# Fifth chunk of the keys by block products inside the product with V, in nine more batches

## The chip, the cores and the metric

One core of one Trainium2 chip. The metric is the device time in microseconds of one execution of the whole program on that core. The kernel before took 913.3 us (median of three runs, 913.17 to 913.3). PE is TensorE, DVE VectorE, ACT ScalarE, POOL GpSimd, SP SyncE, whose queue issues most DMAs.

## What is computed

Cross-attention of 16 batches with 100 queries of 640 columns (8 heads of 80), on 718 keys of 384 columns, plus a second attention over 4 extra tokens. Cut to what matters:

```python
query = hidden_states @ Wq
keyt = enc @ Wk                      # 718 keys, 384 -> 640
valt = enc @ Wv
hs = _mha(query, keyt, valt)         # softmax over 718 keys, 8 heads
ca_q1 = einsum('btc,th->bch', ca, Wq_ca)[:, indices, :]
ca_hs1 = _mha(ca_q1, residual, residual)
ca_hs2 = _mha(ca_hs1 @ Wq, ca @ Wk_ca, ca @ Wv_ca)
out = (hs + ca_hs2) @ Wout + b_out + residual
```

All of it is float32.

## The kernel before

One loop runs over the batches b = 0 to 15. The order of the instructions in it is written by hand for every engine; each engine takes its own queue in order and waits by semaphores.

A batch in PE's order: the scores of b in three thirds (`scores`, L784; tile `st[0..2]`, two key blocks of 120 by 800 columns each), the tokens' product z (`softmax2`, L1026), then the keys of batch b + 1 (`Keys`, four of the five chunks of 128 columns) and the values of b (`Values`) by block products that need fewer multiplications (Strassen-like: 15 products in place of 18, on sums of the inputs that POOL makes in `enc_sums` and on sums of the weights). Their results go from the PSUM banks to `kT` and `vs`: the first to reach a place is copied by ACT, the later ones are added by DVE (L421, L423).

The fifth chunk of the keys (columns 512 to 639, `kT[:, 4]`) is made in two ways:

- `last_keys(b + 1)` (L720): nine plain products of 128x128 by 240 columns (3 thirds of the keys, 3 chunks of 128 of the 384), L702, into a two-bank tile, and two ACT copies. This is used in nine batches: 0, 1, 2, 4, 6, 8, 10, 12 and 14.
- `Chunk(b + 1)` (L730): the 15 block products, each only 64 columns wide, in the eight steps of `K4_PLAN` (L117). Two of a step stand in the two halves of the PE array's columns and run side by side; only the product D stands alone, cut into two halves of 120 keys. Bank `one` holds A (upper half) and B (lower half), bank `two` holds C, D and E. A bank's sum is read after a product and the next product is added on top of it, so that each product has to wait for the read of its bank. `move` (L748) reads with an ACT copy when nothing stands at the place yet, else with a DVE addition. This is used in MIXED batches (3, 5, 7, 9, 11, 13), where steps stand between the queries' products and three of them inside the product with V, before (g, n) = (0, 6), (0, 18) and (1, 6).

The product with V (L1698 to L1723) runs in two halves g of four heads; n counts the 24 pairs (head, key block) of a half, with two products each. In half 0 the pairs are sorted by third, so that `st[0]` is used for n = 0 to 7, `st[1]` for 8 to 15 and `st[2]` from 16 on. The bank `a_ps` is then divided by the sum of the exponentials in its last column (`rs`, L1728, L1730) and the tokens' part `hs2` is added (L1737). y_ps (L969), the tokens' product of batch b + 2, follows on PE; DVE copies `g` from it (L983), ACT then `y_sb` (L987). The next batch's scores follow; the middle third takes the banks of `a_ps` and, as its fourth, that of y_ps.

The softmax of the tokens (`softmax1`, L1009) works on `e1` of the next batch in the stages of `Maximum` (L874): transpose, quad, side, mx, spread, over, then the subtraction `less`; `softmax1(n)` does n stages of these. With `scalar` the stage spread is done by ACT (two copies, L917) and mx needs two operations in place of four, with `fine` side and mx are stages of their own. `exponentials1` is ACT's exponential of `e1`.

In batches 3, 6, 8, 11 and 13 (those behind a batch in PAIRS) the output projection of two row blocks is done first, `project_pair` (L1244): nine products in 18 matmuls, DVE reads (`read`, L1272) and three POOL operations (L1280, L1283, L1284), whose results the last two groups of products use. POOL does the tokens' `values2` (L1101, L1108) before them.

Of the kernel before, what the change touches and what calls it, by code (L numbers as in the profile page):

```python
# [8 lines left out]
F32 = mybir.dt.float32  # L9
# [6 lines left out]
NH, D = 8, 80  # L16
# [125 lines left out]
def kernel(  # L142
# [56 lines left out]

    def scores_tile(name):  # L200
        return main.tile([P, 2, ROWS], F32, tag="st", name=name, bufs=NP)

# [115 lines left out]
    )  # L318
    halves = [t[:, u] for t in [scores_tile(f"wq_{i}") for i in range(NP)] for u in range(2)]
    room = halves.pop()  # L320
# [409 lines left out]
    class Chunk:  # L730


        def __init__(self, b, enc):
            self.enc = enc
            one, two = psum1(f"k4_psA_{b}"), psum1(f"k4_psC_{b}")
            half = P // 2
            self.at = {
                "A": [(one, 0, 0, 0, KT)],
                "B": [(one, half, 0, 0, KT)],
                "C": [(two, half, 0, 0, KT)],  # L740
                "D": [(two, i * half, KT, i * KN, KN) for i in range(2)],
                "E": [(two, 0, 0, 0, KT)],
            }
            self.one = one
            self.plan = iter(K4_PLAN)
            self.opened, self.begun = set(), set()
# [37 lines left out]
    def scores(b, g, tiles):  # L784
# [59 lines left out]
        for i, step in enumerate(steps):  # L844
            step(i == 1)
        st = scores_tile(f"st_{b}_{g}")[:n]
        if g == 1:
# [100 lines left out]
    class Second:  # L948
# [173 lines left out]
    class Last:  # L1122
# [121 lines left out]
        def project_pair(self, between):  # L1244
# [29 lines left out]
            product(b1, [(one[:, :2], w(0, 0))], True)  # L1274
            between(1)
            read(b1, 0, 0)
# [181 lines left out]
    for b in range(B):  # L1458
# [44 lines left out]
        st.append(scores(b, 0, tiles))  # L1503
        if b == 0:
            now.exponentials1()
        nc.vector.tensor_tensor(most[:KN], st[0][:, 0], st[0][:, 1], ALU.max)
        st.append(scores(b, 1, tiles))
# [12 lines left out]
        if b == 0:  # L1520
# [22 lines left out]
            less = subtract(2)  # L1543
            exponential(2)
# [5 lines left out]
            second.softmax1(4)  # L1550
        elif b + 1 < B:
# [69 lines left out]
            if not late:  # L1621
                subtract(2)
                exponential(2)
            if not mixed:
                last_keys(b + 1, enc)
            if b + 2 < B:
# [3 lines left out]
            if last.b in PAIRS:  # L1630
                if not mixed:
                    second.softmax1(3)
                last.project_pair(second.softmax1 if mixed else lambda n: None)
                if last.b == max(PAIRS):
# [3 lines left out]
                    )  # L1638
            if not mixed:
                second.softmax1(8)  # L1640
# [50 lines left out]
        held = b in MIXED and not second.less  # L1691
        if 0 < b < B - 1 and not held:
            second.exponentials1()

        mine.hs = hs = hs_sb
        hs2 = now.hs2
        mixed = b in MIXED
        a_pss = [psumk(f"a_ps_{b}_{g}") for g in (1, 0)][::-1] if mixed else None  # L1698
        for g in range(2):
            a_ps = a_pss[g] if mixed else psum1(f"a_ps_{b}_{g}")  # L1700
            a_v = a_ps[:S, : 4 * (D + 1)].rearrange("p (h e) -> p h e", e=D + 1)

# [3 lines left out]
            for n, (h, i) in enumerate(order):  # L1706
                if mixed and (g, n) in ((0, 6), (0, 18), (1, 6)):
# [7 lines left out]
                for lo, hi in QC:  # L1715
# [7 lines left out]
                    )  # L1723
            if b == 0 and g == 1:
                second.softmax1()
                second.exponentials1()
            rs = small.tile([S, 4], F32, tag="rs", name=f"rs_{b}_{g}")
            nc.vector.reciprocal(rs.unsqueeze(2), a_v[:, :, D : D + 1])  # L1728
            cols = slice(4 * g * D, 4 * (g + 1) * D)
            nc.vector.tensor_tensor(  # L1730
                hs[:S, cols].rearrange("p (h d) -> p h d", h=4),
                a_v[:, :, :D],
                rs.unsqueeze(2).to_broadcast([S, 4, D]),
                ALU.mult,
            )
            if b:
                nc.vector.tensor_tensor(hs[:S, cols], hs[:S, cols], hs2[:, cols], ALU.add)  # L1737
        mine.hs2 = hs2
# [65 lines left out]
```

## Time and profile before

| | before |
|---|---|
| median of the runs | 913.3 us (913.17 to 913.3) |
| the profiled execution's own time | 913.33 us |
| its span | 911.6 us |
| granted TensorE clock | 1.0 |
| L702, nine stretches in the loop | 3.65 us each |
| block products L760, six MIXED batches | 192 matmul records |

The profile gives one execution. A float32 product leaves two records on PE. Rows of a view in order of time begin with start and duration in microseconds; rows of groups end with busy time in us, mean ns of one, and idle time before them with what ended it.

### The profile page before, as it was taken

The page shows a single profiled execution, that of the slowest core. Times are in us where ns is not written, and L with a number is a line of the kernel's source. Part 1 is how long each engine was busy: PE and PEld are TensorE (multiplying, and loading weights), DVE is VectorE, ACT ScalarE, POOL GpSimd, SP SyncE. Part 2 cuts the span into 40 slices and gives each one's busy share as a digit, 9 for nine tenths or more (in the row PEclk, how much of TensorE's full clock was granted, in tenths as well). Part 3 has the DMA queues.
Part 4 walks back from the last instruction along what each step waited for, and adds up shares of the span by engine and source line. Part 5 has one row for each costly group of instructions (what it writes and reads, how often), then busy time and mean ns, then how long its engine had stood idle before and what let it go on. Part 6 is the DMA issues. An engine that isn't in the chain of part 4 may idle for free.

```text
span 911.6 us, 28003 instructions
## 1 busy us (share of the span) xinstructions
PE 904.9 (99%) x12046; PEld 755.5 (83%) x12046; DVE 719.5 (79%) x1174; ACT 455.0 (50%) x874; POOL 711.5 (78%) x684
## 2 busy tenths in 40 slices
PE   9999999999999999999999999999999999999998
PEld 6988889797797978888798787988879788797966
DVE  3669795989859898785988869889895898849883
ACT  2244533747437473653737436374743737436441
POOL 8587999787878879696896959958897688977623
PEclk9999999999999999999999999999999999999999
DMA  8822111031301202130121301103230031300110
GB/s 268 283 81 68 48 50 50 30 100 53 111 4 47 84 34 73 55 104 32 48 61 54 104 33 53 55 25 106 53 83 32 24 107 53 97 31 29 56 50 34
DMA packets 50583, 62.96 MB, mean 69 GB/s; under 512 B 13682, under 2 KB 37810, under 8 KB 50460
## 3 DMA queue, kind: packets, MB, share of 16 engines
q1 hardware_dynamic: 48812, 59.18, 21.3%
q8 instruction: 95, 1.56, 0.7%
q10 hardware_dynamic: 1024, 1.15, 0.4%
q0 software_dynamic: 624, 0.85, 0.4%
q14 instruction: 28, 0.23, 0.1%
HBM read 55.59 MB, written 5.57 MB: 67 GB/s over the span
## 4 chain that ended last, share of the span: by engine, by line
PE 96%; DVE 2%; DMA 0%; ACT 0%; issue 0%; ACTq 0%; DVEq 0%
PE a_ps L1716 12%; PE s_ps L799 12%; PE v_psA L450 11%; PE v_psB L450 9%; PE k_psA L481 9%; PE k_psB L481 7%; PE o_ps L1261 5%; PE kT_ps L702 4%; PE v_psC L450 4%; PE k_psC L481 3%; PE q_ps L618 2%; PE q_ps L560 2%; PE v_psD L450 2%; PE v_psE L450 2%; PE k_psA L760 2%; PE v_ps L391 1%
## 5 line engine op out<-in xcount | busy, mean ns | idle before, releaser
L997 POOL TENSOR_TENSOR e<-ca,g 100x800 f32<-100x800 f32 x64 | 99.3, 1563 | 92.5 <-ACT kT L423 53.9
L516 POOL TENSOR_TENSOR enc<-enc 128x240 f32<-128x240 f32 x144 | 113.2, 796 | 11.6 <-DMA enc<-in_enct 4.5
L1480 DVE TENSOR_TENSOR st<-st,over 120x1600 f32<-120x1600 f32 x48 | 119.0, 2482 | 0.0
L1716 PEld LDWEIGHTS a_ps<-vs,st 120*36 120x36 f32 (+3 forms) x3072 | 111.7, 125 | 5.8 <-issue 3.4
L1716 PE MATMUL a_ps<-vs,st 120*36 120x81 f32 (+3 forms) x3072 | 114.7, 233 | 0.0
L450 PE MATMUL v_psA<-wv_sb,enc 128*120 128x320 f32 x352 | 109.3, 433 | 0.0
L1108 POOL TENSOR_TENSOR hs<-hs,hs 100x640 f32<-100x640 f32 x48 | 94.8, 1975 | 3.8
L1101 POOL TENSOR_TENSOR hs<-vb,p 100x640 f32<-100x640 f32 x64 | 90.7, 1428 | 8.7 <-issue 4.7
L481 PE MATMUL k_psA<-enc,wk_sb 128*128 128x240 f32 x384 | 95.2, 370 | 0.1
L1004 POOL TENSOR_TENSOR e<-e,e 100x800 f32<-100x800 f32 x48 | 91.8, 1913 | 3.8
L450 PE MATMUL v_psB<-wv_sb,enc 128*120 128x320 f32 x296 | 91.8, 433 | 0.0
L1488 ACT ACTIVATE st<-st 120x1600 f32<-120x1600 f32 x48 | 73.9, 1539 | 33.9 <-DVE st L1480 33.6
L450 PEld LDWEIGHTS v_psA<-wv_sb,enc 128*120 128x120 f32 x352 | 64.2, 183 | 25.0 <-DVE vs L421 0.5
L481 PEld LDWEIGHTS k_psA<-enc,wk_sb 128*128 128x128 f32 x384 | 71.6, 190 | 16.0 <-DVE wk_sb L546 0.5
L1492 DVE TENSOR_TENSOR most<-most,st 120x800 f32<-120x800 f32 x64 | 67.0, 1047 | 14.9 <-ACT st L849 13.7
L481 PE MATMUL k_psB<-enc,wk_sb 128*128 128x240 f32 x320 | 78.0, 366 | 0.3 <-DVE sm L1083 0.3
L799 PE MATMUL s_ps<-qp,kT 64*64 64x100 f32 (+1 forms) x3072 | 73.1, 248 | 0.0
L450 PEld LDWEIGHTS v_psB<-wv_sb,enc 128*120 128x120 f32 x296 | 54.1, 183 | 21.9 <-DVE vs L421 0.4
L799 PEld LDWEIGHTS s_ps<-qp,kT 64*64 64x64 f32 (+1 forms) x3072 | 66.9, 130 | 5.4 <-issue 4.2
L1176 ACT COPY hsT<-turned_hs 32x160 f32<-32x160 f32 (+7 forms) x244 | 67.7, 278 | 3.0
L481 PEld LDWEIGHTS k_psB<-enc,wk_sb 128*128 128x128 f32 x320 | 60.7, 190 | 8.6 <-issue 0.7
L423 ACT COPY vs<-v_psA 120x640 f32<-120x640 f32 x45 | 31.2, 693 | 65.1 <-PE v_psA L450 64.9
(209 smaller groups left out, 1897.7 us busy)
## 6 DMA issues: line engine op xcount, KB each, us to landing
vb<-va_d SPq DMA_DIRECT2D x62, 250.0 KB
enc<-in_enct SPq DMA_DIRECT2D x30, 240.0 KB
enc<-in_enct SPq DMA_DIRECT2D x15, 360.0 KB
xT<-in_xt SPq DMA_DIRECT2D x8, 500.0 KB
rest<-in_enct SPq DMA_DIRECT2D x31, 120.0 KB
xn<-in_x SPq DMA_DIRECT2D x11, 320.0 KB
out<-xn SPq DMA_DIRECT2D x11, 320.0 KB
ca<-in_cas SPq DMA_DIRECT2D x16, 156.2 KB
```

What stands on the lines that cost most here:

```text
L450: nc.tensor.matmul(at[0][j][:KN, : H // 2], a_form(self.enc, f)[:, j * KN : (j + 1) * KN], wv_there.get(f, wv_sb[:, W_AT[f]]), start=first ...
L481: nc.tensor.matmul(at[:, i * KT : (i + 1) * KT], wk_sb[:, W_AT[f], i], a_form(self.enc, f), start=(first and i == 0), stop=last, skip_grou ...
L516: nc.gpsimd.tensor_tensor(out, left, right, op)
L799: nc.tensor.matmul(s_ps[at][k0:k1, cols], w, rhs, start=not begun & {(at, k) for k in range(k0, k1, 32)}, stop=last, skip_group_check=True,)
L997: first = nc.gpsimd.tensor_tensor(to, self.ca[:, t, :].unsqueeze(1).to_broadcast([S, NH, S]), g[:, :, t].unsqueeze(2).to_broadcast([S, NH, ...
L1004: made = nc.gpsimd.tensor_tensor(e, e, to, ALU.add)
L1101: first = nc.gpsimd.tensor_tensor(to, self.vb[t][:S].rearrange("p (h d) -> p h d", h=NH), p2[:, :, t].unsqueeze(2).to_broadcast([S, NH, D] ...
L1108: nc.gpsimd.tensor_tensor(sums, sums, to, ALU.add)
L1176: nc.scalar.copy(self.hsT(r)[32 * m : 32 * m + 32, :, first - lo : end - lo], turned[32 * i : 32 * i + 32, :, m, first - at : end - at],)
L1480: return nc.vector.tensor_tensor(st[i], st[i], top.over[:KN].unsqueeze(1).to_broadcast([KN, 2, ROWS]), ALU.subtract,)
L1488: nc.scalar.activation(st[i], st[i], AF.Exp, scale=SCALE)
L1716: nc.tensor.matmul(a_v[lo:hi, h % 4], st[i // 2][: KEYS[i], i % 2, h * S + lo : h * S + hi], block(i, h // 4)[: KEYS[i], h % 4], start=(i ...
```

## The change

The fifth chunk is made by `Chunk` in the nine other batches too. PLAIN names six of these, 0, 2, 4, 10, 12 and 14; the rest are 1, 6 and 8. Two steps of the plan stand before the product with V and six in it, at n = 9, 14, 19, 23 of half 0 and n = 3 and 16 of half 1. The first two steps are swapped in these batches, so that D comes first. Around it:

- In PLAIN batches the exponential of `st[2]` stands behind the first two steps, the stages of `softmax1` between the later ones, and the head sums of both halves behind them; the rest of `softmax1` comes after y_ps and `exponentials1` in the next batch, behind its first scores. `softmax1` there has `scalar` and `fine`.
- In batches 6 and 8 (and the MIXED ones behind a pair, as before) `project_pair` calls `softmax1` between its products; the first of the calls is made only in MIXED batches. The later stages follow the projection. In 1, 6 and 8 `exponentials1` stands at the last step.
- In all batches but 15 `a_ps` is in the pool of banks psumk. From batch 1 on, division and addition are one fused operation for each head (100x80), eight of them in place of two multiplications and two additions.
- The three score tiles are fixed tiles; rows 96 to 127 of the first are filled with the lowest number once, so that the maximum runs over 128 rows and ACT's copy of `low` in every batch (L1502) is gone.

```diff
+PLAIN = [b for b in range(B - 1) if b not in (1, *MIXED) and b - 1 not in PAIRS]
...
+    sts = [main.tile([P, 2, ROWS], F32, name=f"st_{i}") for i in range(NP)]
...
-            self.plan = iter(K4_PLAN)
+            swap = b - 1 not in MIXED
+            self.plan = iter(K4_PLAN[1::-1] + K4_PLAN[2:] if swap else K4_PLAN)
...
+                after = self.b - 1
                 self.top = Maximum(
-                    e1, f"1_{self.b}", self.b - 2 in PAIRS, self.b - 1 in MIXED
+                    e1,
+                    f"1_{self.b}",
+                    after - 1 in PAIRS or after in PLAIN,
+                    after in (*MIXED, *PLAIN) or after - 1 in PAIRS,
                 )
...
             product(b1, [(one[:, :2], w(0, 0))], True)
-            between(1)
+            if self.b + 1 in MIXED:
+                between(1)
             read(b1, 0, 0)
...
+        st.append(scores(b, 0, tiles))
+        if b == 0 or b - 1 in PLAIN:
+            now.exponentials1()
         most = wide(f"most_{b}")
-        nc.scalar.copy(most[96:], low[96:].to_broadcast([P - 96, ROWS]))
...
             if not late:
                 subtract(2)
+            if not late and b not in PLAIN:
                 exponential(2)
-            if not mixed:
-                last_keys(b + 1, enc)
...
             if last.b in PAIRS:
-                if not mixed:
-                    second.softmax1(3)
-                last.project_pair(second.softmax1 if mixed else lambda n: None)
+                last.project_pair(second.softmax1)
...
-            if not mixed:
+            if not mixed and b not in PLAIN:
                 second.softmax1(8)
...
+        if b < B - 1 and not b in MIXED:
+            chunk = Chunk(b + 1, enc)
+            chunk.go(2)
+        if b in PLAIN:
+            exponential(2)
...
+        a_pss = [(psumk if b < B - 1 else psum1)(f"a_ps_{b}_{g}") for g in (1, 0)][::-1]
...
+        if b in MIXED:
+            steps = (0, 6), (0, 18), (1, 6)
+        else:
+            steps = (0, 9), (0, 14), (0, 19), (0, 23), (1, 3), (1, 16)
...
+                if b in PLAIN and (g, n) in ((0, 23), (1, 6)):
+                    second.softmax1(1)
+                if b in PLAIN and (g, n) == (1, 16):
+                    second.softmax1(1)
+                if b < B - 1 and (g, n) in steps:
                     chunk.go()
+                    if b not in MIXED and (g, n) == steps[-1]:
+                        if b in PLAIN:
+                            second.softmax1(2)
+                        else:
+                            second.exponentials1()
...
+                for h in range(4):
+                    part = slice((4 * g + h) * D, (4 * g + h + 1) * D)
+                    nc.vector.scalar_tensor_tensor(
+                        hs[:S, part],
+                        a_v[:, h, :D],
+                        rs[:, h : h + 1],
+                        hs2[:, part],
+                        ALU.mult,
+                        ALU.add,
+                    )
...
+        if b in PLAIN:
+            second.softmax1()
```

More of the change, by code (lines that the diff above doesn't have):

```diff
@@ L318 @@
     )
-    halves = [t[:, u] for t in [scores_tile(f"wq_{i}") for i in range(NP)] for u in range(2)]
+    halves = [t[:, u] for t in sts for u in range(2)]
     room = halves.pop()
@@ L845, in scores @@
             step(i == 1)
-        st = scores_tile(f"st_{b}_{g}")[:n]
+        st = sts[g][:n]
         if g == 1:
@@ L1500 @@
             now.softmax1()
-        most = wide(f"most_{b}")
-        nc.scalar.copy(most[96:], low[96:].to_broadcast([P - 96, ROWS]))
[L1503 to L1506, printed above, removed]
+            nc.scalar.copy(
+                sts[0].rearrange("p a r -> p (a r)")[96:],
+                low[96:].to_broadcast([P - 96, 2 * ROWS]),
+            )
+        st.append(scores(b, 0, tiles))
+        if b == 0 or b - 1 in PLAIN:
+            now.exponentials1()
+        most = wide(f"most_{b}")
+        nc.vector.tensor_tensor(most, sts[0][:, 0], sts[0][:, 1], ALU.max)
         st.append(scores(b, 1, tiles))
@@ L1549 @@
             enc_sums(enc_next)
-            second.softmax1(4)
         elif b + 1 < B:
@@ L1691 @@
         held = b in MIXED and not second.less
-        if 0 < b < B - 1 and not held:
+        if b in MIXED and not held:
             second.exponentials1()
+        if b < B - 1 and not b in MIXED:
[3 more added lines that the diff above has]
+            exponential(2)
         mine.hs = hs = hs_sb
         hs2 = now.hs2
-        mixed = b in MIXED
-        a_pss = [psumk(f"a_ps_{b}_{g}") for g in (1, 0)][::-1] if mixed else None
+        a_pss = [(psumk if b < B - 1 else psum1)(f"a_ps_{b}_{g}") for g in (1, 0)][::-1]
+        a_vs = [
+            a_ps[:S, : 4 * (D + 1)].rearrange("p (h e) -> p h e", e=D + 1)
+            for a_ps in a_pss
+        ]
+        if b in MIXED:
+            steps = (0, 6), (0, 18), (1, 6)
+        else:
+            steps = (0, 9), (0, 14), (0, 19), (0, 23), (1, 3), (1, 16)
         for g in range(2):
-            a_ps = a_pss[g] if mixed else psum1(f"a_ps_{b}_{g}")
-            a_v = a_ps[:S, : 4 * (D + 1)].rearrange("p (h e) -> p h e", e=D + 1)
+            a_v = a_vs[g]
             order = [(h, i) for h in range(4 * g, 4 * g + 4) for i in range(len(KC))]
@@ L1723 @@
                     )
[L1724 to L1737, printed above, removed]
+            if b in PLAIN and g == 0:
+                continue
+            for g in range(2) if b in PLAIN else (g,):
+                a_v = a_vs[g]
+                rs = small.tile([S, 4], F32, tag="rs", name=f"rs_{b}_{g}")
+                nc.vector.reciprocal(rs.unsqueeze(2), a_v[:, :, D : D + 1])
+                cols = slice(4 * g * D, 4 * (g + 1) * D)
+                if b == 0:
+                    nc.vector.tensor_tensor(
+                        hs[:S, cols].rearrange("p (h d) -> p h d", h=4),
+                        a_v[:, :, :D],
+                        rs.unsqueeze(2).to_broadcast([S, 4, D]),
+                        ALU.mult,
+                    )
+                    continue
+                for h in range(4):
[5 more added lines that the diff above has]
+                        hs2[:, part],
+                        ALU.mult,
+                        ALU.add,
+                    )
         mine.hs2 = hs2
```

5 lines of the change are left out of this document (removed).

## The prediction

> **What bounds the kernel.** The page first: span, engines, chain of waits.
>
> ```profile
> span 911.6 us, 28003 instructions
> PE 904.9 (99%) x12046; PEld 755.5 (83%) x12046; DVE 719.5 (79%) x1174; ACT 455.0 (50%) x874; POOL 711.5 (78%) x684
> PE 96%; DVE 2%; DMA 0%; ACT 0%; issue 0%; ACTq 0%; DVEq 0%
> ```
>
> TensorE (PE) is busy for 99% of the span and makes 96% of the chain: hardly anything that another engine does shows now. So a product removed is worth its whole time, and every wait that the change puts into PE's queue costs its whole length. Then the chain in order of time, where one of the nine batches (batch 4) has:
>
> ```profile
> 300.98 3.65 PE kT_ps L702 x18
> 304.63 6.91 PE a_ps L1716 x191
> ```
>
> The fifth chunk of the next batch's keys takes 3.65 us, then come the products with V. The instructions of the same batch by engine, in order of time:
>
> ```profile
> 300.82 1.38 PE L702 MATMUL kT_ps<-enc,wk 128*128 128x240 f32 x6
> 304.56 6.98 PE L1716 MATMUL a_ps<-vs,st 120*64 120x81 f32 x192
> 311.36 0.93 PE L969 MATMUL y_ps<-m,xT 128*36 128x72 f32 x20
> 312.21 1.60 PE L799 MATMUL s_ps<-qp,kT 64*64 64x100 f32 x64
> 313.74 1.63 PE L799 MATMUL s_ps<-qz,kT 32*120 32x200 f32 x32
> ...
> 301.02 0.56 ACT L423 COPY kT<-k_psA 128x480 f32<-128x480 f32 x1
> 302.67 1.54 ACT L1488 ACTIVATE st<-st 120x1600 f32<-120x1600 f32 x1 [1.09 <-DVE st L1480]
> 313.44 0.37 ACT L987 COPY y_sb<-y_ps 100x256 f32<-100x256 f32 x1 [2.41 <-DVE g L983]
> ...
> 299.71 2.87 DVE L1480 TENSOR_TENSOR st<-st,over 120x1600 f32<-120x1600 f32 x1
> 302.50 1.00 DVE L890 STREAM_TRANSPOSE turned<-e 128x800 f32<-128x800 f32 x1
> 303.53 0.99 DVE L892 TENSOR_REDUCE quad<-turned 128x25 f32<-128x800 f32 x1
> 304.56 0.71 DVE L895 TENSOR_REDUCE side<-quad 32x25 f32<-32x25 f32 x4
> ```
>
> The 3.65 us of L702 hold nothing that waits, and they cover VectorE's subtraction (to 302.58) and ScalarE's exponential (to 304.21), which the products with st_2 need. That cover goes.
>
> **What the block products cost.** Batch 3 already does its fifth chunk this way:
>
> ```profile
> 246.73 0.38 PE L760 MATMUL k_psC<-enc,w_sums 128*64 128x120 f32 x4
> 246.94 1.86 PE L651 MATMUL q_ps<-xT,wq_sb 128*64 128x200 f32 x20
> 256.87 0.37 PE L760 MATMUL k_psA<-enc,w_sums 128*64 128x240 f32 x1
> 257.28 1.87 PE L1716 MATMUL a_ps<-vs,st 120*64 120x81 f32 x48
> 258.98 0.57 PE L760 MATMUL k_psA<-enc,w_sums 128*64 128x240 f32 x4
> ...
> 246.95 0.72 ACT L752 COPY kT<-k_psA 64x240 f32<-64x240 f32 x2 [2.87 <-PE k_psA L760]
> 247.68 0.52 ACT L752 COPY kT<-k_psC 64x120 f32<-64x120 f32 x2
> 257.49 0.36 ACT L752 COPY kT<-k_psA 128x240 f32<-128x240 f32 x1 [0.84 <-PE k_psA L760]
> ...
> 259.60 0.83 DVE L750 TENSOR_TENSOR kT<-k_psA,kT 64x240 f32<-64x240 f32 x2 [1.31 <-PE k_psA L760]
> ```
>
> A pair takes 256.87 to 257.28, 0.41 us; D takes 0.21. Seven pairs and D: 3.04 (at 0.405, as L702's 3.65 for nine products gives for one) against 3.65: **0.61 less in each of nine batches, -5.5 us**. Between two pairs 48 records take 1.70, so one (h, i) of the products with V (four records) takes 0.142. The Trainium skill ("TensorEngine Tiling (Array Packing)", Key Properties) says that a change of tiling mode drains TensorE; the rows do not show it, since pair and 48 records together keep 2.10 from 256.87 to 258.98, but it is a rival below.
>
> What a read costs a pair behind it, from the same rows: a copy starts 0.62 after its pair's start (256.87 to 257.49) and takes 0.36, an addition starts as late (258.98 to 259.60) and takes 0.42. With some 0.05 to return (an estimate: ScalarE starts that long after a matmul record's end), PE may reuse the bank 1.03 to 1.08 after the pair's start. The L702 way had two copies behind nine products; now there are 14 reads, and each bank is written again after a few (h, i).
>
> **Batch 4 laid out**, T = 300.82. D and the first pair end at T+0.62, nine (h, i) at 1.89. There step (0, 9) writes bank B, which ScalarE must have copied: it is busy with k_psA to T+0.76, then copies D (0.52) and A, B (0.72), to 2.00: PE waits 0.15. (0, 14) comes at 3.16 and finds its addition done; the exponential, now behind the four copies, ends at 3.55, before (h, i) 16 at 3.85; (0, 19) at 4.28 just fits. (0, 23) follows 0.41 and four (h, i) later, 0.97 after (0, 19), but A's addition needs 1.08: wait 0.11. (1, 3) is 0.97 behind (0, 23), whose copy needs 1.03: wait 0.06. (1, 16) is late enough. Products with V end at T+10.2, against 10.54 before (311.36). So **step waits: 0.17 in each of nine batches and about 0.15 more in the six where ScalarE still has work in front (1, 2, 4, 10, 12, 14; batch 0 below): +2.4 us**; bounds 1.2 (half of it) and 3.5.
>
> VectorE now does the tokens' maximum in pieces between the additions: transpose to T+6.4, quad to 8.9, side to 9.6, two additions of the last step to 10.4, two mx to 11.1. Only then come the head sums of both halves, two reciprocals (as short as the first row below, 0.2 each) and eight fused operations of 100x80, which no row shows:
>
> ```profile
> L983 DVE COPY g<-y_ps 100x32 f32<-100x32 f32 x15 | 2.7, 178 | 0.0
> L750 DVE TENSOR_TENSOR kT<-k_psA,kT 64x240 f32<-64x240 f32 x24 | 9.7, 402 | 8.3 <-PE k_psA L760 7.8
> ```
>
> So each costs 0.18 to 0.40; by size nearer the short one, I take 0.22. A price for it is in the Trainium skill ("Vector Engine (DVE) Microarchitecture Reference", 5.2 Measured stream behaviour on trn2): 75 ns and 1.04 ns per column, an estimate of 0.16, by which the next term would be about 0.5. Head sums end at T+13.3, the copy of g and then y_sb (0.37) at 13.85. Scores of batch 5 want y_ps's bank again at its second third's fourth bank: before, at 312.21 + 1.53 + 0.78 + 0.3 = 314.8, 3.4 after the products with V, now T+13.6: wait 0.3 in 2, 4, 10, 12. Batch 14 has no y_ps in between, its head sums are wanted 0.85 earlier: 0.85. **+2.0 us**; bounds 0.5 (at 0.18) and 9 (at 0.40).
>
> **Batches 6 and 8.** Before:
>
> ```profile
> 402.80 1.38 PE L702 MATMUL kT_ps<-enc,wk 128*128 128x240 f32 x6
> 406.44 2.85 PE L1261 MATMUL o_ps<-wout_sb,hsT 128*128 128x320 f32 x10
> 416.23 6.98 PE L1716 MATMUL a_ps<-vs,st 120*64 120x81 f32 x192
> ...
> 406.28 0.65 DVE L904 TENSOR_REDUCE mx<-side 32x25 f32<-32x100 f32 x2
> 416.33 0.89 DVE L1272 TENSOR_TENSOR xn<-o_ps,xn 128x320 f32<-128x320 f32 x2 [0.58 <-PE o_ps L1261]
> ...
> 407.35 1.73 ACT L917 COPY spread<-mx 64x800 f32<-64x800 f32 x2
> ...
> 409.24 0.73 POOL L1280 TENSOR_TENSOR hsT<-hsT,hsT 128x256 f32<-128x256 f32 x1
> 411.20 1.54 POOL L1284 TENSOR_TENSOR wout<-wout,wout_sb 128x640 f32<-128x640 f32 x1
> ```
>
> Two things move. First, between(1) and between(2) now do transpose, quad and side inside the pair projection, but mx and spread come out of softmax1(8) behind it: on VectorE behind the reads of the last o_ps (0.2 + 0.89 after its products), mx 0.65, then the spread on ScalarE 1.73, and only behind that in ScalarE's queue the chunk's copies (0.52 + 0.72). They end 4.8 after the chunk's start; step (0, 9) wants them at 1.9. **Wait 2.9, twice: +5.8 us**, by the order of the queues alone. Second, the projection starts 3.65 earlier, GpSimd does not: L1284 can follow L1280 (409.24) and L1283 at best to 412.2, while the last two products of the projection, 18 of equal length in 9.7, would start at 402.85 + 8.6 = 411.5. **Wait 0.7, twice: +1.4**; bounds 0 and 2.
>
> **Batch 0.**
>
> ```profile
> 85.41 1.38 PE L702 MATMUL kT_ps<-enc,wk 128*128 128x240 f32 x6
> ...
> 86.46 0.64 DVE L421 TENSOR_TENSOR kT<-k_psC,kT 128x480 f32<-128x480 f32 x1
> ...
> 86.07 1.54 ACT L1488 ACTIVATE st<-st 120x1600 f32<-120x1600 f32 x1
> ```
>
> The chunk's first pair takes the bank of k_psC, read until 87.1, and ScalarE is at an exponential until 87.6, then come the copies, 1.24: step (0, 9) at 88.9 instead of 87.4. **+1.5**.
>
> Removed: ScalarE's copy of low and the separate additions of hs, all beside PE: nothing. The rest tile is free earlier, its DMA may land earlier: nothing. Restart of PE behind each of some 35 waits: 0 to 0.14 (no row shows one), I take 0.03: **+1.0**, bounds 0 and 4.9.
>
> **Sum**, against this execution's own time of 913.33 us (span 911.6 and 1.7 around it; the median of the runs is 913.3): -5.5 + 2.4 + 2.0 + 5.8 + 1.4 + 1.5 + 1.0 = +8.6, **922.0 us**.
>
> **Rivals.** (a) Only the queue-order waits remain (6, 8 and 0); the small ones are met, as my 0.05 to 0.15 margins may be too strict: -5.5 + 5.8 + 1.5, 915.1. For it: the 1.08 against 0.97 is a tenth of a us. Against: it recurs in nine batches. (b) Other side: the copies are not late. Place: ScalarE's queue at step (0, 9); from the point where they end within 1.9 of the chunk's start the reads keep pace everywhere and the whole 5.5 stays: 907.8. Against: in 6 and 8 the spread in front ends at 3.6 by measured durations. (c) VectorE's lateness is carried on: behind a plain batch the tokens' second transpose and subtraction, two operations of L890's kind, stand in front of the next batch's maxima, one of them no longer under the products with V, so these come some 1 us later; where additions of the odd batch then hold a bank, six times up to 1.2 us: 929. Against it, in batch 5 VectorE waits for PE and can catch up:
>
> ```profile
> 331.65 0.82 DVE L421 TENSOR_TENSOR vs<-v_psA,vs 120x640 f32<-120x640 f32 x1 [0.58 <-PE v_psA L450]
> ```
>
> (d) The drain by the skill's rule: at 0.16 (a record's 0.37 less half a pair's 0.41) at both sides of six steps in nine batches, +17, 939; the 2.10 above speak against it.
>
> **Chances.** Forecast 0.58, (a) 0.19, (b) 0.06, (c) 0.14, (d) 0.03. The range 914.8 to 928.5 takes in (a) and the lower bounds of the terms, and part of (c). About 0.2% (1.8 us) can be told from no change: faster 0.06 is (b); same 0.07 is the lower part of (a); slower 0.87.
>
> **What would show it.** In batches 6 and 8 PE stands idle for about 3 us before L761's second products, released by ScalarE's copy L753; a stall there missing breaks the forecast. Short waits before L761 at (0, 23) and (1, 3), released by VectorE and ScalarE; a wait of s_ps on y_sb behind 2, 4, 10 and 12; the products L761 themselves 3.04 a batch. PE's share of the span falls below 99%. If it does not, (b) holds.

## Result and profile after

The changed kernel takes 926.79 us (median of four runs, 924.97 to 927.56), the kernel before 913.23 on the same chip: ratio 1.0147, 95% interval 1.0129 to 1.0164. It is slower by 13.6 us; the forecast was 922.0, slower by 8.6, with a range of 914.8 to 928.5.

The page of after, the lines that answer to those shown of before (span, busy time of the engines, chain of waits):

```profile
span 925.8 us, 28438 instructions
PE 911.2 (98%) x12172; PEld 749.1 (81%) x12172; DVE 723.0 (78%) x1288; ACT 462.5 (50%) x907; POOL 703.9 (76%) x684
PE 85%; POOL 7%; DVE 5%; ACT 1%; DMA 1%; issue 1%; ACTq 0%; DVEq 0%; POOLq 0%
```

PE's share of the chain falls from 96% to 85%: other engines now show. PE's busy time even rises, from 904.9 to 911.2, although products were removed. The records did not get longer: the products with V are 3072 records of 233 ns on average before and 234 after, and yet their busy time goes from 114.7 to 126.9. A record starts some 0.035 us behind the last one and runs on for 0.23, so a stretch that is cut into more pieces counts the end of each piece, and a wait shorter than a record counts as busy. Nine batches with six cuts each make 54 more ends of some 0.2 us, 11 of the 12 us. So busy time can't price the change, and places have to be compared. The table does so: time from a batch's first score record to that of the next (for batch 15 to the end of the span), less the same time in the profile of before (the last column is a control, explained with its run below).

| batch | after | 6, 8 as before | subtraction late | x load first | y ahead | steps apart | plain only | all four | before, x load late |
|---|---|---|---|---|---|---|---|---|---|
| 0 | 3.10 | 3.07 | 3.07 | 0.98 | 3.09 | 2.83 | -0.20 | 0.77 | 1.95 |
| 1 | 0.52 | 0.52 | 0.53 | 0.53 | 0.62 | -0.04 | -0.11 | -0.01 | -0.11 |
| 2 | -0.26 | -0.15 | -0.11 | -0.13 | -0.27 | -0.22 | -0.37 | -0.39 | 0.08 |
| 3 | 0.67 | 0.78 | 0.52 | 0.63 | 0.08 | 0.83 | 0.36 | 0.91 | 0.07 |
| 4 | -0.27 | -0.10 | -0.26 | -0.26 | -0.27 | -0.52 | -0.51 | -0.51 | 0.01 |
| 5 | 0.41 | 0.42 | 0.39 | 0.40 | 0.00 | 0.69 | 0.23 | 0.20 | 0.12 |
| 6 | 5.27 | 0.60 | 1.02 | 5.42 | 5.41 | 3.76 | -0.02 | 0.51 | -0.01 |
| 7 | -0.40 | -0.41 | -0.03 | -0.40 | -0.40 | -0.41 | -0.41 | 0.36 | -0.41 |
| 8 | 4.34 | 0.20 | 1.12 | 4.30 | 4.37 | 3.83 | 0.01 | 0.49 | 0.00 |
| 9 | -0.16 | -0.17 | 0.14 | -0.16 | -0.16 | -0.17 | -0.17 | -0.16 | -0.16 |
| 10 | -0.26 | -0.23 | -0.26 | -0.26 | -0.22 | -0.51 | -0.51 | -0.51 | 0.00 |
| 11 | 0.41 | 0.25 | 0.42 | 0.50 | 0.63 | 0.58 | 0.32 | 0.79 | -0.01 |
| 12 | -0.26 | -0.26 | -0.26 | -0.16 | -0.26 | -0.52 | -0.52 | -0.51 | 0.00 |
| 13 | 0.57 | 0.47 | 0.50 | 0.47 | 0.42 | 0.95 | 0.27 | 0.59 | 0.09 |
| 14 | -0.27 | -0.27 | -0.27 | -0.27 | -0.27 | -0.53 | -0.52 | -0.52 | -0.01 |
| 15 | 0.57 | 0.55 | 0.57 | 0.84 | 0.55 | 0.83 | 0.82 | 0.86 | -0.08 |

Four things are to be seen in the column of after: batches 6 and 8 lose 9.6 us of the 14.2 by which the span grew; batch 0 loses 3.1; a plain batch gains 0.26, and the odd batch behind it loses 0.41 to 0.67, more than that.

A plain batch in order of time, batch 4 of after (start, duration; PE, then VectorE, then ScalarE):

```profile
305.10 0.43 PE L761 MATMUL k_psC<-enc,w_sums 128*64 128x120 f32 x4
305.35 0.57 PE L761 MATMUL k_psA<-enc,w_sums 128*64 128x240 f32 x4
305.76 1.43 PE L1739 MATMUL a_ps<-vs,st 120*64 120x81 f32 x36
307.02 0.37 PE L761 MATMUL k_psC<-enc,w_sums 128*64 128x240 f32 x1
...
309.73 0.74 PE L1739 MATMUL a_ps<-vs,st 120*64 120x81 f32 x16
310.38 0.42 PE L761 MATMUL k_psA<-enc,w_sums 128*64 128x240 f32 x1
...
317.66 2.03 PE L800 MATMUL s_ps<-qz,kT 32*120 32x200 f32 x32
...
315.06 0.65 DVE L905 TENSOR_REDUCE mx<-side 32x25 f32<-32x100 f32 x2
...
317.28 0.93 DVE L1764 SCALAR_TENSOR_TENSOR hs_sb<-a_ps,rs,hs 100x80 f32<-100x80 f32 x4
318.12 0.18 DVE L984 COPY g<-y_ps 100x32 f32<-100x32 f32 x1
...
318.33 0.37 ACT L988 COPY y_sb<-y_ps 100x256 f32<-100x256 f32 x1 [0.86 <-DVE g L984]
```

Step (0, 9) at 307.02 waits for nothing: nine (h, i) took 1.26, 0.14 each. At (0, 23) 16 records fill 0.65 instead of 0.57 (four at 0.142): a wait of 0.08, and the pair that had to wait takes 0.46 (310.38 to 310.84, where a pair takes 0.41). At (1, 3) the same shows: 0.06 of waiting and a pair of 0.46. Then the scores: 32 records of `qz` take 2.03 where before they took 1.63. In their stretch y_sb is read until 318.70; that is the 0.40 that batch 5 loses, all of it at this one place. The eight fused operations take 0.93 for four, 0.23 each (0.22 was taken); by the price of the Trainium skill ("Vector Engine (DVE) Microarchitecture Reference", 5.2 Measured stream behaviour on trn2) that the prediction quotes it would be 0.16, so here the measurement decides against it.

Batch 6 of after, same view and columns, with the idle time before a row and what ended it in brackets:

```profile
416.66 1.34 PE L1266 MATMUL o_ps<-wout,hsT 128*128 128x320 f32 x4 [0.42 <-POOL wout L1290]
417.94 0.43 PE L761 MATMUL k_psC<-enc,w_sums 128*64 128x120 f32 x4
...
421.85 0.62 PE L761 MATMUL k_psC<-enc,w_sums 128*64 128x240 f32 x2 [1.82 <-ACT kT L753]
422.60 0.56 PE L761 MATMUL k_psA<-enc,wk 128*64 128x240 f32 x1
...
424.24 0.66 PE L761 MATMUL k_psA<-enc,w_sums 128*64 128x240 f32 x1
...
419.53 1.73 ACT L918 COPY spread<-mx 64x800 f32<-64x800 f32 x2 [10.00 <-DVE mx L905]
421.28 0.52 ACT L753 COPY kT<-k_psC 64x120 f32<-64x120 f32 x2
421.82 0.72 ACT L753 COPY kT<-k_psA 64x240 f32<-64x240 f32 x2
...
418.85 0.65 DVE L905 TENSOR_REDUCE mx<-side 32x25 f32<-32x100 f32 x2
421.29 1.01 DVE L926 STREAM_TRANSPOSE over<-spread 128x800 f32<-128x800 f32 x1 [1.79 <-ACT spread L918]
422.33 1.41 DVE L1024 TENSOR_TENSOR e<-e,over 100x800 f32<-100x800 f32 x1
423.78 0.41 DVE L751 TENSOR_TENSOR kT<-k_psA,kT 64x240 f32<-64x240 f32 x1
```

This is the stall that the prediction named: ScalarE's spread stands in front of the chunk's copies. PE idles 1.82 at step (0, 9), released by L753; the second product of the step needs the second copy, starts at 422.60, and is 2.7 late, where 2.9 was foretold. But the stall does not end there. The addition of the pair's sums starts only at 423.78, behind the tokens' second transpose and subtraction on VectorE, so the next step starts at 424.24, 5.6 us after the start of the products with V (418.60) where it needs 2.4: 3.2 late. In batch 8 it is the same (535.56 to 541.20).

Batch 6 has a second loss that batch 8 lacks. The granted clock drops to half, from 422.73 for 3.41 us, and a record of the block products takes up to 0.66 in place of 0.37. Three microseconds of after, then the same of the run with the steps further apart, below (start:end, length, busy time of PE, PEld, DVE, ACT and POOL, granted clock, DMA):

```profile
423.00:426.00 3.00, 3.00 (x36) 2.62 (x34) 1.81 (x4) 0.00 (x0) 2.84 (x4) 0.50 0.03 8
423.00:426.00 3.00, 2.67 (x53) 2.20 (x52) 1.62 (x5) 0.00 (x0) 2.84 (x5) 1.00 0.03 8
```

From the chunk's start to the last product with V batch 6 takes 14.65 and batch 8, at full clock, 13.71; so some 0.9 to 1.0 of the 5.27 is the clock. The two runs below that also have the drop there (x load first, y ahead) lose 5.4 in batch 6 and 4.3 to 4.4 in batch 8; the run without it (steps apart) loses 3.8 in both. What sets the drop off was not tried; the profile of before has none in the loop.

And batch 0, ahead of the chunk. First before (SyncE's queue, VectorE, GpSimd), then after (the same, and PE):

```profile
39.65 0.52 SPq L218 DMA_DIRECT2D xT<-in_xt  x1
47.18 0.31 SPq L959 DMA_DIRECT2D ca<-in_cas  x1
...
67.34 3.23 DVE L1492 TENSOR_TENSOR most<-most,st 120x800 f32<-120x800 f32 x2
...
67.56 4.41 POOL L997 TENSOR_TENSOR e<-ca,g 100x800 f32<-100x800 f32 x2 [0.56 <-issue]
```

```profile
47.37 0.31 SPq L960 DMA_DIRECT2D ca<-in_cas  x1
47.73 0.38 SPq L218 DMA_DIRECT2D xT<-in_xt  x1
...
67.72 4.98 DVE L1498 TENSOR_TENSOR most<-most,st 120x800 f32<-120x800 f32 x2
...
68.79 3.04 POOL L998 TENSOR_TENSOR e<-ca,g 100x800 f32<-100x800 f32 x2
...
77.02 1.05 PE L481 MATMUL k_psA<-enc,wk_sb 128*128 128x240 f32 x4 [1.64 <-DVE kT L421]
```

The planner that orders the work ahead of the loop put the load of x behind that of `ca`, which waits for GpSimd; the load now comes at 47.73 and not at 39.65. GpSimd's product starts 1.2 us later, VectorE's two maxima take 4.98 in place of 3.23, and PE waits 1.64 at 77.02. Nothing in the diff speaks of this load.

### The profile page after: what moved, and what is told of

The parts are those of the page before. It is cut to its first block, busy times and chain, and to the rows that moved or that the text cites. A ratio compares the mean times of both kernels' runs of the same rounds, so it can differ in the third digit from the quotient of the medians.

```text
span 925.8 us, 28438 instructions
## 1 busy us (share of the span) xinstructions
PE 911.2 (98%) x12172; PEld 749.1 (81%) x12172; DVE 723.0 (78%) x1288; ACT 462.5 (50%) x907; POOL 703.9 (76%) x684
## 4 chain that ended last, share of the span: by engine, by line
PE 85%; POOL 7%; DVE 5%; ACT 1%; DMA 1%; issue 1%; ACTq 0%; DVEq 0%; POOLq 0%
PE s_ps L800 11%; PE a_ps L1739 10%; PE v_psA L450 9%; PE v_psB L450 8%; PE k_psA L481 7%; PE k_psB L481 6%; PE k_psA L761 4%; PE o_ps L1266 3%; PE v_psC L450 3%; PE k_psC L481 2%; PE q_ps L618 2%; PE q_ps L560 2%; PE v_psD L450 2%; PE v_psE L450 2%; PE v_ps L391 1%; PE q_psA L618 1%
## 5 line engine op out<-in xcount | busy, mean ns | idle before, releaser
L1739 PEld LDWEIGHTS a_ps<-vs,st 120*64 120x64 f32 (+3 forms) x3072 | 122.2, 125 | 10.5 <-issue 0.8
L1739 PE MATMUL a_ps<-vs,st 120*64 120x81 f32 (+3 forms) x3072 | 126.9, 234 | 0.0
L516 POOL TENSOR_TENSOR enc<-enc 128x240 f32<-128x240 f32 x144 | 106.8, 752 | 12.3 <-DMA enc<-in_enct 5.3
L918 ACT COPY spread<-mx 64x800 f32<-64x800 f32 x54 | 46.4, 858 | 46.8 <-DVE mx L905 46.5
```

Source lines behind the costliest of these rows:

```text
L516: nc.gpsimd.tensor_tensor(out, left, right, op)
L1739: nc.tensor.matmul(a_v[lo:hi, h % 4], st[i // 2][: KEYS[i], i % 2, h * S + lo : h * S + hi], block(i, h // 4)[: KEYS[i], h % 4], start=(i ...
```

## Experiments

**Batches 6 and 8 as before.** `ALONE` is (6, 8):

```diff
+            if b in ALONE:
+                last_keys(b + 1, enc)
+                second.softmax1(3)
...
-                last.project_pair(second.softmax1)
+                last.project_pair((lambda n: None) if b in ALONE else second.softmax1)
...
-        if b in MIXED and not held:
+        if b in (*MIXED, *ALONE) and not held:
...
-        if b < B - 1 and not b in MIXED:
+        if b < B - 1 and b not in (*MIXED, *ALONE):
```

> Batches 6 and 8 make the fifth chunk of the keys in one piece in front of the pair projection, with the tokens' maximum where it stood; the other seven batches stay changed. By the profile of after, 6 to 9 together lost 9.05 us (5.27 and 4.34, less 0.40 and 0.16 that 7 and 9 gained). If all of that comes from the order inside 6 and 8, this run takes 926.8 - 9.05 = 917.7. If only the prediction's terms for these two batches belong to them (5.8 + 1.4 + 0.3 - 1.2 = 6.3) and the rest is a lateness brought in from earlier batches, it takes 920.5. If the loss is simply carried to the next batches, 925 or more.

916.37 us, ratio to before 1.0033 (1.002 to 1.0045). The two batches' 9.6 us fall to 0.8, and batches 7 and 9 stand where the control has them. The loss belongs to these two batches; none of it is carried out to later ones. What is left, 0.60 and 0.20, arises in the tokens' product z; for batch 6 the profile names no engine that it waits for.

**ScalarE's copies ahead of the spread.**

```diff
-            if not mixed and b not in PLAIN:
+            if b == 1:
                 second.softmax1(8)
...
             chunk.go(2)
+        if b in (6, 8):
+            second.softmax1(8)
```

> In batches 6 and 8 the chunk's first copies go into ScalarE's queue ahead of the tokens' spread; nothing else moves. The prediction's own term (only ScalarE's copies are late, 2.9 us in each batch) expects the stall at step (0, 9) to go and 926.8 - 5.8 = 921.0. The rival: the two vector operations behind the spread (second transpose and subtraction, 2.4 us together) still stand ahead of the chunk's additions in VectorE's queue, and since the spread now starts about 1.2 us later, the additions start no earlier than at 424.0 (423.8 in after): the wait goes from step (0, 9) to step (0, 14) at nearly full length, and the run takes 926 to 927.

928.33 us, ratio 1.0146 (1.0124 to 1.0168): nothing gained against 1.0147. Batch 6 of this run, in order of time:

```profile
423.64 0.63 PE L761 MATMUL k_psA<-enc,w_sums 128*64 128x240 f32 x4 [3.10 <-DVE kT L751]
...
417.81 0.52 ACT L753 COPY kT<-k_psC 64x120 f32<-64x120 f32 x2 [8.86 <-PE k_psC L761]
...
418.97 1.72 ACT L918 COPY spread<-mx 64x800 f32<-64x800 f32 x2
...
420.73 1.01 DVE L926 STREAM_TRANSPOSE over<-spread 128x800 f32<-128x800 f32 x1 [1.84 <-ACT spread L918]
421.77 1.37 DVE L1024 TENSOR_TENSOR e<-e,over 100x800 f32<-100x800 f32 x1
423.18 0.41 DVE L751 TENSOR_TENSOR kT<-k_psA,kT 64x240 f32<-64x240 f32 x1
```

The copies are on time now and step (0, 9) does not wait. PE stops one step later, for 3.10, and the releaser has changed from ScalarE to VectorE: its addition stands behind the transpose and the subtraction, which themselves wait for the spread. Step (0, 14) starts 6.30 after the chunk's start, in after (417.94 to 424.24) as in this run (417.34 to 423.64), so the stall has its full length. The time of the run says less than this place: its five executions spread from 923.96 to 929.67, and in the profiled one the granted clock is at half from 424.29 for 3.41 us and from 540.34 for 6.83 us, where batches 6 and 8 lose 5.78 and 6.66 (in after 5.27 and 4.34). The prediction's own term, ScalarE's queue alone, expected 921.0 and falls here.

**The same, and the subtraction late.** In place of `softmax1(8)` the run does `softmax1(2, True)` there (mx and spread), and the rest behind step (1, 3):

```diff
+                    if b in (6, 8) and (g, n) == (1, 3):
+                        second.softmax1()
```

> As the run before this one, and the tokens' second transpose and subtraction of batches 6 and 8 go behind step (1, 3). If the two queues' order (ScalarE's spread, then VectorE's transpose and subtraction) is the whole stall behind the chunk's first pair, 4.2 us in batch 6 and 3.5 in batch 8 go (the 4.87 and 4.18 that 6 with 7 and 8 with 9 lost, plus the 0.61 less of products, less 1.0 of waits for GpSimd in the projection and about 0.3 of short waits): 919.1. If the waits for GpSimd in the projection are the larger part, the gain is under 4 and the run takes 923 or more.

918.22 us, ratio 1.0047 (1.0034 to 1.006). Batch 6:

```profile
416.35 1.34 PE L1266 MATMUL o_ps<-wout,hsT 128*128 128x320 f32 x4 [0.41 <-POOL wout L1290]
417.62 0.43 PE L761 MATMUL k_psC<-enc,w_sums 128*64 128x120 f32 x4
...
420.66 0.62 PE L761 MATMUL k_psA<-enc,w_sums 128*64 128x240 f32 x4
...
426.38 1.00 DVE L926 STREAM_TRANSPOSE over<-spread 128x800 f32<-128x800 f32 x1
```

Both queues together were the stall: 3.22 us go in batch 8 and 4.25 in batch 6 (5.27 to 1.02), where the half clock is gone too, about 1.0. Some 0.7 of the 7.5 comes back in batches 7 and 9, at their scores. GpSimd's wait in the projection stays, 0.41 at L1290. The time that the projection takes in after, 407.18 to 417.94, is 10.76 where before it was 9.79 (406.44 to 416.23), so GpSimd costs 0.97 in a batch.

**The x load ahead of ca.**

```diff
-    xT_at = [None]
+    xT_at = [load_x(1)]
...
-            x_next = xT_at[0] if b % 2 else load_x(p + 1)
+            x_next = xT_at[0] if b % 2 or b == 0 else load_x(p + 1)
```

> The first load of the next pair's x (500 KB) is issued ahead of the load of the tokens' ca, as in before; after has it behind, where it waits for GpSimd's product at 47.4 us and then shares the DMA engines with the encoder's load. If that is why GpSimd's sums of batch 0 ended 1.8 us later, why VectorE's maximum then met GpSimd's product (4.98 us instead of 3.23) and why TensorE waited 1.64 at 77.0, about 2.1 us go: 924.7. If the longer maximum comes from the change's own edits (maximum over 128 rows, the filled rows), the run stays at 926.8.

925.4 us, ratio 1.0126 (1.0112 to 1.0139); batch 0 loses 0.98 and not 3.10. Its two maxima and GpSimd's product are back at the lengths that they have in before:

```profile
67.01 3.23 DVE L1498 TENSOR_TENSOR most<-most,st 120x800 f32<-120x800 f32 x2
...
67.23 4.40 POOL L998 TENSOR_TENSOR e<-ca,g 100x800 f32<-100x800 f32 x2 [0.56 <-issue]
```

The 2.12 us in the profile agree with the 2.1 expected; of the median 1.4 went, and the two intervals overlap. The run of before with the same load late, below, tests this from the other side.

**The copies of y_ps between the two halves' head sums.**

```diff
             for g in range(2) if b in PLAIN else (g,):
+                if b in PLAIN and g == 1 and b + 2 < B:
+                    second_next.products()
+                    second_next.copy()
...
-        if b + 2 < B:
+        if b + 2 < B and b not in PLAIN:
             second_next.products()
```

> In the plain batches (0, 2, 4, 10, 12, 14) the copies of g and y_sb out of y_ps are issued between the head sums of the two halves, not behind both. The prediction's reason for the loss in 3, 5, 11 and 13 (the scores want y_ps's bank, y_sb is read late behind mx and the head sums) expects the step of 0.40 us that each of them shows at its scores to go: 1.6 less, 925.2. The rival: the second half's sums, now 0.2 later, hold their own bank for the scores, and the wait only changes its releaser: 926.8, with the wait ended by VectorE's sums.

926.4 us, ratio 1.0134 (1.0118 to 1.0149). Batch 4 of this run:

```profile
316.84 1.63 PE L800 MATMUL s_ps<-qz,kT 32*120 32x200 f32 x32
...
316.67 0.37 ACT L988 COPY y_sb<-y_ps 100x256 f32<-100x256 f32 x1
```

In batches 3 and 5 the wait is gone (1.63 again, as before), 0.59 and 0.41 less. In 11 and 13 there remain 0.63 and 0.42. The rival accounts for 0.25 in batch 11, where the scores wait for VectorE's sums; the rest of 11, and 0.31 of 13, arise in the last third of the scores, where the profile names no engine. Half right.

**Two steps further apart.**

```diff
-            steps = (0, 9), (0, 14), (0, 19), (0, 23), (1, 3), (1, 16)
+            steps = (0, 9), (0, 14), (0, 19), (1, 0), (1, 5), (1, 16)
```

> The fourth and fifth step of the block products go from (0, 23) and (1, 3) to (1, 0) and (1, 5) in the batches that are not mixed. The prediction's short waits (0.11 for VectorE's addition, 0.06 for ScalarE's copy, some 0.17 in each) should go: batches 2, 4, 10, 12, 14 gain 0.43 each and not 0.26, the run takes about 925.5. The rival, that the 0.34 us missing from the nominal 0.61 in each of them is what starting and ending a step costs and not a wait, expects 0.26 as before, 926.8.

924.45 us, ratio 1.0116 (1.01 to 1.0132). Batches 4, 10, 12 and 14 gain 0.51 to 0.53 and not 0.26 (batch 2 stays at 0.22): waits they were, with the longer pairs behind them 0.26 in each. Of the 0.61 at most 0.09 is left for starting and ending six steps. Batch 1, where the prediction expected a gain and after lost 0.52, is even with it (-0.04). Batches 6 and 8 gain 1.5 and 0.5: 0.5 in each, since their additions have more time, and in batch 6 the half clock, which this profile does not have there. But 5, 11, 13 and 15 lose 0.2 to 0.4 more: the head sums end where they did, and the scores, now earlier, wait longer for them.

**Before with the x load behind ca.** The load stands behind `Second(1, xT)` in the code, and both loads are kept in that order; all else is the kernel before.

> The kernel of before with nothing changed but the order of two loads: that of the next pair's x goes behind that of the tokens' ca, as the planner put it in after. If this order alone made the 2.1 us that after loses ahead of the chunk of batch 0, this run takes 913.6 + 2.1 = 915.7, with VectorE's two maxima near 67 at about 5 us instead of 3.23. If it needs the change's other edits too, 913.6.

915.07 us, ratio 1.0013 (1.0 to 1.0026). Batch 0 loses 1.95, and VectorE shows the same long pair of maxima as after:

```profile
68.23 4.97 DVE L1497 TENSOR_TENSOR most<-most,st 120x800 f32<-120x800 f32 x2
```

So the order of two loads alone does it. This run is also a control for the table, as batches 1 to 15 hold the same instructions as before: they differ by up to 0.12, and 7 and 9 by -0.41 and -0.16, as in most other columns. That is a peculiarity of the one profiled execution of before and no gain.

**The change in the five later plain batches alone, with three repairs** (x load first, y_ps ahead, steps apart):

```diff
+ALONE = (0, 1, 6, 8)
-PLAIN = [b for b in range(B - 1) if b not in (1, *MIXED) and b - 1 not in PAIRS]
+PLAIN = [b for b in range(B - 1) if b not in (*ALONE, *MIXED)]
```

> The change in the plain batches 2, 4, 10, 12 and 14 alone (0, 1, 6 and 8 make their chunk in one piece as before), with the x load ahead of ca, the copies of y_ps between the halves' sums and the two steps moved. Against before: five times 0.43 to 0.61 less, batch 15 some 0.2 to 0.6 more, the waits for y_sb gone: 911.0 to 912.2 where before takes 913.6. The rival, that batches 6 and 8 with fused head sums keep the 0.6 and 0.2 that they lost in the run with both as before, expects 912 to 913.

913.12 us, ratio 0.9997 (0.9988 to 1.0005): no difference that can be told, where 911.0 to 912.2 was expected. Batches 6 and 8 lose nothing (-0.02 and 0.01), so the rival's reason falls too. The plain batches gain 0.37 to 0.52 each; 3, 5, 11 and 13 lose 0.23 to 0.36 and 15 loses 0.82. What still holds the scores of batch 5 is the second half's head sums, until 313.79:

```profile
313.03 1.85 PE L801 MATMUL s_ps<-qz,kT 32*120 32x200 f32 x32
...
312.86 0.93 DVE L1781 SCALAR_TENSOR_TENSOR hs_sb<-a_ps,rs,hs 100x80 f32<-100x80 f32 x4
```

**First half's sums early.** Behind the previous run, with the code of one half's sums put into `sums(g)`:

```diff
+                if b in PLAIN and (g, n) == (1, 6):
+                    sums(0)
...
             if b in PLAIN:
                 if b + 2 < B:
                     second_next.products()
                     second_next.copy()
+                second.softmax1(2)
+            sums(g)
```

> As plain_only_repaired, and in batches 2, 4, 10, 12, 14 the first half's head sums go ahead of quad, behind step (1, 5), and mx goes behind the copies of y_ps. In that run batches 3, 5, 11, 13 still lost 0.23 to 0.36 and 15 lost 0.83, with the second half's sums ending 2.3 us after the scores' start, where the scores want their bank at about 2.1. If that bank alone holds TensorE, the sums now end at about 2.05, the odd batches lose under 0.1 each and 15 under 0.3, and the run takes about 1.7 us less than plain_only_repaired: 0.998 of before. The rival: quad, side and mx, 0.6 to 1 later, make the tokens' exponential late for z_ps, and what the scores gain is lost there: 1.000.

917.1 us, ratio 1.0042 (1.0028 to 1.0057). A miss: 3, 11, 13 and 15 lose about 1.5. The second half's sums end at 315.19, 2.54 after the scores' start (312.65), not 2.05: in front of them VectorE now has the chunk's last addition (312.68 to 313.09) and mx (313.35 to 314.02), and everything behind is later. Where it shows, in batch 3 (weight loads of PE: waited for, us in total, times, longest):

```profile
PEld k_psC L482 <- DVE vs L422: 0.9, 1, 0.9
PEld z_ps L1037 <- ACT st L851: 0.5, 1, 0.5
```

The wait that the rival foretold at z_ps is there, and a larger one stands 30 us into the odd batch, at a bank whose addition VectorE does too late: the lateness is carried that far.

**The whole change with all four repairs.**

> The whole change in all nine batches with the four repairs together: ScalarE's copies ahead of the spread and the subtraction late in 6 and 8, the x load ahead of ca, the two steps moved, the copies of y_ps between the halves' sums. If the causes are separate, they add up: 918.2 (the run with the subtraction late) less 2.1 (x load), less about 1.0 (steps: 0.26 in five batches, 0.56 in batch 1, 0.27 in batch 0, less 1.2 that the odd batches then lose at their scores), less about 1.0 (y_ps, in 3 and 5): 914.1, ratio 1.0005 against before. What would be left over before: about 0.7 in batch 0, 0.7 in each of 6 and 8 (GpSimd in the projection), 0.2 to 0.8 in the odd batches, against 0.5 gained in each of 2, 4, 10, 12, 14. If a repair only uncovers the next wait, 916 to 918.

916.15 us, ratio 1.0028 (1.0018 to 1.0038); 914.1 was expected. The 13.6 us of the change come down to 2.5. The 2.0 that are missing are not missing between the profiles: the span falls from 918.6 (subtraction late) to 914.5, by the 4.1 expected, but the profiled execution of the run with the subtraction late took 920.4, the longest of its five, where their median was 918.2. So the x load's 2.1 does not seem to be paid in every execution of a kernel that has it late. The times of before with the load late point the same way: four of ten are 912.5 to 913.1 and six 914.9 to 917.7. That it is the meeting in batch 0 that comes and goes was not shown, as there is one trace of each kernel.

Against this, batches 3 and 7 lose 0.91 and 0.36, more than foretold. In batch 7 it is the scores, 0.77 against the control: they wait for y_sb, which stands behind the subtraction that was moved late in batch 6. Batch 3 shows the same place as the run before (PE, then its weight loads):

```profile
PE k_psC L481 <- DVE vs L421: 0.4, 1, 0.4
...
PEld k_psC L481 <- DVE vs L421: 0.8, 1, 0.8
```

Why batch 3 meets this wait here and not in the plain-only run, where batch 2 is the same, was not settled.

## Why the prediction was right, and where it was not

**The direction and its cause** were right: the gain in products is small, and waits put into PE's queue cost more. The number came out 4.8 short, and two things that the prediction did not lay out, the x load and the half clock, make 3.1 of the profiled execution. By its terms:

- Products, -5.5: right. With the steps apart a plain batch gains 0.52 of the 0.61; shown.
- Step waits, +2.4: the places (0, 23) and (1, 3) right, 0.15 in a plain batch for 0.17, shown by moving the steps. The further 0.15 at (0, 9) does not occur: ScalarE's copies end 1.83 after the chunk's start, not 2.00.
- Bank of y_ps, +2.0: right. 0.40 in each of 3, 5, 11 and 13 (0.3 foretold) and 0.57 behind 14 (0.85). Shown for 3 and 5; in 11 and 13 about as much is lost at other places once the wait is gone.
- Batches 6 and 8, +5.8: the wait for ScalarE was right (2.7 in each for 2.9), but it was taken as the whole and as over when ScalarE's copies end. The two runs with the copies moved show VectorE's transpose and subtraction as a second queue with the same fault, behind the same spread: together 3.2 in each, 6.4 us, and repairing ScalarE's queue alone gains nothing. The half clock in batch 6 adds about 1.0, and the short waits at the later steps, which moving the steps takes away, 0.5 in each. The place to see the second queue stood in the layout, as VectorE's list ended with mx and left out the rest of `softmax1(8)`.
- GpSimd late in the projection, +1.4: 1.9, within its bounds.
- Batch 0's chunk, +1.5: right. With the x load back in place the batch loses 0.98, where -0.61, 0.17 and 1.5 make 1.06.
- Batch 1, taken as a plain batch (-0.29): it lost 0.52, of which the moved steps remove 0.56. The layout was that of a PLAIN batch; in batch 1 the head sums of the first half stand in front of additions in VectorE's queue. That the sums are what is late there was not tried by itself.
- Restarts, +1.0: there, though the prediction had no row for them. A pair behind a wait takes 0.45 or 0.46 and not 0.41, as at 310.38 above; in a plain batch the pairs are 0.16 longer in sum, where 1.0 in nine batches is 0.11, and 0.07 longer once the steps are moved. Together with the step waits that is 0.31 in a plain batch for 0.43: the waits were taken too large, the longer pairs too small, and that the sum lies as near as it does is in part luck.
- Not foreseen: the x load, +2.1 in the profiled execution, shown from both sides. The prediction did not lay out SyncE's queue, since the diff touches no load.
- Not foreseen: the half clock behind the stall of batch 6, about 1.0 in the profiled execution.

In the profile the span grew by 14.1 (14.2 by the page's rounded figures) where the terms add up to 8.6. The 5.5 between them, by place: 1.9 in batch 0 (the load's 2.1), 0.7 in batch 1, 3.1 in 6 and 8 (1.0 the clock, 0.6 the second queue, 0.5 GpSimd, the rest the short waits), 0.6 in the odd batches with a plain one ahead of them (3, 5, 11, 13 and 15) and 0.2 ahead of batch 0, less 0.4 in the other plain batches, which lost less than foretold, and 0.6 in 7 and 9, which is the profile of before.

**The rivals.** (a) and (b) fall: the small waits are there, and the copies are late. (d), the drain that the Trainium skill ("TensorEngine Tiling (Array Packing)", Key Properties) speaks of, falls with the 0.52 gained: six steps switch there and back for at most 0.09. (c), VectorE's lateness carried into the odd batch, is no cause of the main loss, as batch 5 loses its 0.40 at the scores and nothing behind; but it exists: in the profile of after batches 3 and 13 fall back by 0.24 and 0.15 more some 29 us in, at the same bank that costs 0.9 in the run with early sums.

## What to carry to other kernels

When work is put into a bound engine's stream in small steps that need reads in between, lay out every queue that serves these reads, to the end of what stands in front of them: repairing the first queue moved the stall to the second at full length. A small gain in a batch is easily lost in the next one: a bank that the next stage wants was read 0.4 us later here, and that outweighed 0.26. Compare the order of the loads of the two programs even where the diff touches none. And read the granted clock behind a stall: here 1.0 of the 5.3 us that batch 6 lost was the clock and not a queue.

## What the runs showed of the hardware that was not expected

- VectorE's maximum of two tiles in SBUF and GpSimd's product, both on SBUF, shut each other out. Each of them without the other, in the order of time of after (VectorE in batch 5, GpSimd ahead of the loop, beside two additions of VectorE out of PSUM banks):

```profile
323.14 2.02 DVE L1498 TENSOR_TENSOR most<-most,st 120x800 f32<-120x800 f32 x2 [0.93 <-ACT st L850]
...
37.15 3.04 POOL L998 TENSOR_TENSOR e<-ca,g 100x800 f32<-100x800 f32 x2 [6.28 <-DVE g L984]
```

  Where GpSimd started 0.2 after VectorE, they took 3.23 and 4.41; where it started 1.1 after, 4.98 and 3.04: VectorE's excess of 2.96 is the length of GpSimd's two products. The Trainium skill ("SBUF — State Buffer", SBUF: two separate sides) says that an instruction with two SBUF inputs on VectorE and one on GpSimd take a shared port for the whole of an instruction, and that whoever starts first blocks the other. The traces agree that the one blocks the other: both are done 4.6 and 5.0 us after the first start, where one after the other would take 5.06. Which of two close starts wins they do not show: in after VectorE's second maximum starts at 68.73, GpSimd's first product at 68.79, and VectorE pays. A shift of one microsecond decided it here.
- The two halves of the PE array's columns can start apart. At 421.85 and 422.60 in batch 6 of after each product of the step waits for its own copy by ScalarE (they end at 421.80 and 422.54), so the second starts 0.75 after the first, where a pair in step starts within 0.01 us and takes 0.41 in all.
- At a stall in which PE idled 1.82 us the granted clock fell to half for 3.41 us (batch 6 of after); in the run with the copies ahead of the spread it fell for 3.41 and 6.83 us at stalls of 3.10 and 3.09. Stalls of 1.82 in batch 8 of after and in batch 6 of the run with the steps apart went without a drop, so the stall's length alone does not decide.
